# Step 0's part of ten tiles' outputs: made beside the end of step 0 instead of among the outputs at the end

## The chip, the cores and the metric

The kernel runs on one core of a Trainium2 chip. The metric is the device time of one execution in microseconds (us). PE is the matrix engine, PEld its weight loads, DVE, ACT and POOL are the vector, scalar and GpSimd engines, SP is the queue that issues most loads and stores.

## The reference

The input is x (3327 rows of 256, float32) and a sparse 0/1 matrix adj. Two layers follow each other, each with a residual and a layer norm. Layer 0 is a graph attention over adj with a gated update. Its normalised output X is what the change is about, for layer 1 does two steps from it:

```python
Z = 0
Xf = Xa = X
for n in range(2):
    A = top_p_attention(Xa)        # softmax of q k^T, the largest entries up to 0.9 of the sum kept
    Xf = R @ Xf                    # R: (adj + I), rows divided by their sums; sparse
    Xa = A @ Xa
    Z = Z + Xf @ U1[n].T + Xa @ U2[n].T
h = X + Z
out = layernorm(X + layernorm(h) * ln_g + ln_b)
```

So a row's sum before the first norm has five parts: X, two products from step 0 (Xf and Xa after step 0, with U1[0] and U2[0]) and two from step 1. Each part depends on that row alone, once Xf and Xa of the step are known.

## The kernel before

The 3327 rows are 26 tiles of 128 (the last has 127). In time the kernel has these stages: layer 0 (to about 398 us), step 0 of layer 1 (to about 966), step 1 (its products of A and Xa run from 988 to 1568), and the ends (1570 to 1833), where the outputs are made.

**Step 0** (`step_0`) is a pipeline over tiles. A tile's work is a generator, `sparse(t)`, and each call of it is a tick. A new tile enters every EVERY0 = 32 ticks (about 19.4 us in the steady part), and the table ORDER_0 says at which tick of a tile each part stands, from "logits0" at 0 to "qk3" at 180. So some six tiles are in work at once. Parts that matter here, with their names in the profile:

- "xf": the sparse product R X of a tile: POOL gathers the neighbours' rows (`g`), PE sums them (`pxf`), ACT scales to `xf`, SP stores it in `xf_rows` in DRAM.
- "index" and "needed": POOL gathers the rows of X with their keys that the tile needs (`g<-x1k,uidx`), after a small list has gone to DRAM and back (`ulist`, `back`).
- "turned": PE turns the gathered keys (`pk`), ACT copies them (`kg`). "by_nodes weights": PE makes the logits again for these few rows (`plt`), ACT takes the exponential (`w`). "kept": DVE removes those under the limit. "attention": PE sums (`pav`), DVE inverts the sum (`rA`). "xa": ACT writes the tile's Xa into `self.xa`, which holds all tiles in SBUF, and SP stores it in `xa_rows`.
- "qk": PE turns xa (`ptq`) and makes q and k of step 1 (`pq`), ACT copies them.

When the last tile has entered, the pipeline drains. Beside the drain a second generator, `first_1`, makes the logits and the largest entries of step 1's first tile as soon as the k that they need exist (`pl` on PE, copied by ACT).

**Step 1** works through the 26 tiles as dense products of the masked A and Xa (`pt`, `at`, `pav` on PE).

**The ends** (`ends`) have two kinds of work. A few "hard" rows, put aside because their limit needs an exact search, are done in three rounds: a search and a mask on DVE (`bound`, `hard`; the tiles with an h in their names), then transposes `pth`, copies `ath`, products `pavh` and the rows' own outputs `xh` (`hard_end`). Among these stand the outputs of the 26 tiles, one generator `tile_end(t)` each. A tile end loads the tile's Xf and Xa of both steps and X (`xfs`, `xa`, `x`), turns them on PE (`ptxut` for step 0, `ptxvt` for step 1: four transposes each), copies them on ACT (`xtut`, `xtvt`), makes the products on PE into one bank (`pzt`: four for `xtut`, four for `xtvt`, each as two halves U1, U2; then x1 by the identity, `plus`), and hands it to the two norms on DVE, ACT and POOL (`bn..`, `mv..`, `shift..`, and `h`, which lies in columns of qT that are free by then). A new tile end starts at 0.8 per tick; while DVE searches, PE works at tile ends.

On PE, DVE and ACT the order of the instructions is the order in which the program issues them (`manual_schedule`), in step 0 on POOL too. Everything else, SP's queue of loads and stores in particular, is put in order by a scheduler. Each engine takes its instructions strictly in its order.

U1 and U2 are loaded once (`load_u1`, for U1: `kT<-in_U1T_dram`), into columns of kT that step 0's logits have used before. The call stands after step 1's first mask; in SP's queue the scheduler had put it just after the last reading of those columns, and it is issued at 878.56 us.

Buffers that count: PSUM has two banks with the tag "av" (`pav`, `pzt`) and two with "sm" (`ptq`, `pk`, `ptxut` and other small ones); SBUF has two of tag "xf" (rows of Xf and Xa loaded from DRAM), two of tag "own" and four of tag "xt".

Of the kernel before, what the change touches and what calls it, by code (L numbers as in the profile page):

```python
# [9 lines left out]
F32 = mybir.dt.float32  # L10
# [6 lines left out]
P = 128  # L17
N = 3327
D = 256
DC = D // P  # L20
DA = 64
NT = (N + P - 1) // P
# [44 lines left out]
EVERY0 = 32  # L67
# [19 lines left out]
    ) for name in names.split()  # L87
]
AT_0 = {name: tick for tick, name in ORDER_0}

GROUP = (208, 167)
LIST = (40, 72)
# [14 lines left out]
def rows(t):  # L107
    return TAIL if t == NT - 1 else P
# [13 lines left out]
def move_rows(engine, dst, src, r):  # L122

    full = r // 16 * 16
    for a, b in ((0, full), (full, r)):
        if a < b:
            engine.dma_start(dst[a:b], src[a:b])
# [170 lines left out]
class SlowLayer1:  # L298
# [33 lines left out]
    def transposed(self, srcs, r, tag):  # L332

        nc = self.nc
        xt = self.work.tile([P, 2 * DC, P], F32, tag="xt", name=f"xt{tag}")
        pt = self.psm.tile([P, 2 * DC, P], F32, tag="sm", name=f"ptx{tag}")
        for s, a in enumerate(srcs):
            for c in range(DC):
                nc.tensor.transpose(pt[:, s * DC + c, :r], a[:, c * P : (c + 1) * P], self.ident[:r, :r])
        m = len(srcs) * DC  # L340
        nc.scalar.copy(xt[:, :m, :r], pt[:, :m, :r])
        return xt
# [827 lines left out]
class Layer1:  # L1170
# [52 lines left out]
    def setup_0(self, keep, dram):  # L1223
# [16 lines left out]
        self.needed = keep.tile([P, NT], F32, name="needed")  # L1240
        self.ulist = dram.tile([NT, UB * P], F32, name="ulist")

    def sparse(self, t):


        parts = self.parts_0(t)
        at = 0
        for tick, name in ORDER_0:
            while at < tick:
                at += 1  # L1250
                yield
            parts[name]()
# [319 lines left out]

    def step_0(self):

        tiles, first = [], self.first_1()
        self.done = self.phase = 0

        for p in self.p:
            self.nc.vector.memset(p.bitcast(BF16)[:, N : N + 1], -1.0)
        while self.phase < EVERY0 * NT or tiles:  # L1580
            if self.phase % EVERY0 == 0 and self.phase // EVERY0 < NT:
                tiles.append(self.sparse(self.phase // EVERY0))
            for g in list(tiles):
                if next(g, True):
                    tiles.remove(g)
                    self.done += 1
            next(first, None)
            self.phase += 1
        for _ in first:
            pass  # L1590

    def first_1(self):


        while self.phase <= EVERY0 * (NT - 1) + max(AT_0[k] for k in ("sign0", "sign1", "xf")):
            yield
        v = self.item(NT)
        self.item(NT + 1)
        self.fetch(NT)
        v.cand = self.candidates(v.r, GROUP[1], v.tag)  # L1600
        ready, waiting = [], list(range(-(-N // GROUP[1])))
        for pair in self.chunks():
            while self.done * P < min(NT * P, HALF + pair[0][1] + LC):
                yield
            for i in (NT, NT + 1):
                self.some_logits(i, pair)
                yield
            ready += [c for h, s in pair for c in range(h * HALF + s, min(N, h * HALF + s + LC))]
            have = set(ready)
            for g in list(waiting):  # L1610
                if have.issuperset(range(g * GROUP[1], min(N, (g + 1) * GROUP[1]))):
                    waiting.remove(g)
                    self.eights(v.cand, v.l, v.r, GROUP[1], g * GROUP[1], min(N, (g + 1) * GROUP[1]))
            yield

    def transposed(self, srcs, r, tag, kind="xt"):

        nc = self.nc
        xt = self.work.tile([P, 2 * DC, P], F32, tag=kind, name=f"xt{tag}", bufs=4)
        pt = self.psm.tile([P, 2 * DC, P], F32, tag="sm", name=f"ptx{tag}")  # L1620
        for s, a in enumerate(srcs):
            for c in range(DC):
                nc.tensor.transpose(pt[:, s * DC + c, :r], a[:, c * P : (c + 1) * P], self.ident[:r, :r])
        m = len(srcs) * DC
        nc.scalar.copy(xt[:, :m, :r], pt[:, :m, :r])
        return xt

    def chunks(self):

# [263 lines left out]
        yield  # L1893
        self.normalized(h, h, m, r, f"b{tag}")

    def tile_end(self, t):

        nc, r, sh = self.nc, rows(t), self.sh
        on = slice(t * P, t * P + r)
        a = self.work.tile([P, EB, P], F32, tag="m", name=f"xfs{t}").rearrange("p b c -> p (b c)")  # L1900
        xa2 = self.work.tile([P, D], F32, tag="xf", name=f"xa2_{t}")
        x1 = self.work.tile([P, D], F32, tag="xf2", name=f"x1_{t}")[:r]

        spare = lambda k: sh.qT[:r, k * D : (k + 1) * D]
        h, xb = spare(t % 9), spare(9 + t % 3)
        move_rows(nc.sync, a[:r, :D], sh.xf_rows[on, :], r)
        move_rows(nc.sync, a[:r, D : 2 * D], sh.xf2_rows[on, :], r)
        move_rows(nc.sync, xa2[:r], sh.xa2_rows[on, :], r)
        move_rows(nc.sync, x1, sh.x1_rows[on, :], r)
        yield  # L1910
        xts = [
            self.transposed((a[:r, :D], self.xa[:r, t, :]), r, f"ut{t}"),
            self.transposed((a[:r, D : 2 * D], xa2[:r]), r, f"vt{t}"),
        ]
        yield
        pz = self.pac.tile([P, 512], F32, tag="av", name=f"pzt{t}")
        for n, xt in enumerate(xts):
            self.output_terms(pz, xt, n, (0, 1), r, n == 0, False)
        self.plus(pz, x1, r)
        yield  # L1920
        rest = self.output_rows(pz, [xb], h, r, f"t{t}")
        for k, _ in enumerate(rest):
            if k == 2:
                move_rows(nc.sync, xb, sh.xb_rows[on, :], r)
            yield
        move_rows(nc.sync, self.out[on, :], h, r)
# [255 lines left out]
    def ends(self, bounds):  # L2182


        ends, open_ends, queue = [self.tile_end(t) for t in range(NT)], [], []
        ticks = 0

        def tick():


            nonlocal ticks
            ticks += 1
            if ends and (NT - len(ends) < 0.8 * ticks or not searching):
                open_ends.append(ends.pop(0))
            for g in open_ends[::-1]:
                if next(g, True):
                    open_ends.remove(g)

        def more():
            if queue and next(queue[0], True):  # L2200
                queue.pop(0)
            tick()

            for _ in range(2):
                for g in bounds:
                    if not next(g, True):
                        break

        def start(k):
            yield from self.hard_q(k)  # L2210
            for pair in self.chunks():
                yield
                self.hard_exp(k, pair)
            bounds.append(self.coarse_bound(k, CUTS[:COARSE], self.items[f"h{k}"].other))

        def end(k):
            yield from self.hard_end(k)
            open_ends.append(self.items[f"h{k}"].end)

        queue.append(start(2))  # L2220
        searching = True
        for k in range(HARD):
            if k:
                for _ in bounds[k - 1]:
                    pass
                for _ in self.bound(k, CUTS[COARSE:]):
                    more()
            for _ in self.hard(k):
                more()
            queue.append(end(k))  # L2230
        searching = False
        while queue or open_ends or ends:
            more()
        for k in range(HARD):
            self.hard_store(k)

    def run(self):
        nc, sh, total = self.nc, self.sh, STEPS * NT
# [4 lines left out]
        with self.tc.manual_schedule(engines=engines):  # L2243
# [5 lines left out]
            self.list_3(NT)  # L2249
            self.mask(NT)  # L2250
            self.put_aside_1(NT)
            self.load_u1()
            for i in range(NT, total):
                if i + 2 < total:
                    self.item(i + 2)
# [140 lines left out]
```

## Time and profile before

| | us |
|---|---|
| median of 3 runs | 1832.16 |
| lowest, highest | 1831.43, 1836.68 |
| the profiled execution | 1834.81 |
| its span | 1833.0 |
| PE busy (share of the span) | 1554.1 (85%) |
| DVE busy | 1396.6 (76%) |
| POOL busy | 1074.6 (59%) |
| ACT busy | 1056.6 (58%) |
| xa of tiles 23, 24, 25 written from | 943.45, 953.69, 963.98 |
| last copy of the hard rows' sum (xh) | 1795.79 |

The mean clock that PE was granted is 0.926 of full speed. The profile's other times are those of the one profiled execution, from the start of its span. In a line of the timeline stand the start, the length, the engine, the line of the program, the operation with its output and inputs, the number of instructions, and in brackets the engine's idle time before it with what it waited for.

### The profile page before, as it was taken

The numbers are of one execution on the slowest core, as the hardware profiler recorded it, in microseconds if no ns is written. First come the engines' busy times: TensorE is split into PE (matmuls) and PEld (weight loads), VectorE is DVE, ScalarE is ACT, GpSimd is POOL, SyncE is SP. The second block draws the span as 40 slices with busy tenths as digits, with TensorE's granted clock in tenths as the row PEclk, the third lists the DMA queues.
The fourth block names the chain that finished last, engine by engine and source line by source line (L and its number), as shares of the span: only waits on it lengthen the run. The fifth ranks groups of instructions, "written<-read, shape, count | busy, mean of one in ns | idle before, by whom it ended". The sixth has DMA issues, their size and how long they took to land. (4 is left out here: it accounts for less than half of the span.)

```text
span 1833.0 us, 28746 instructions
## 1 busy us (share of the span) xinstructions
PE 1554.1 (85%) x8425; PEld 1086.2 (59%) x8425; DVE 1396.6 (76%) x4759; ACT 1056.6 (58%) x2388; POOL 1074.6 (59%) x1774
## 2 busy tenths in 40 slices
PE   6499999976888898888766999999999889788992
PEld 4255555543555555555444777777777656677872
DVE  5788887447787788778628999999999877967741
ACT  3366666745667676766624555555555546558454
POOL 2477777624565566565463656665665583666654
PEclk9799999977899889889888999999999999899996
DMA  8877773322333333333330111111111120213321
GB/s 263 288 262 234 238 229 97 83 67 75 93 98 100 92 92 97 101 89 97 88 82 24 50 52 52 51 48 50 47 47 50 50 64 18 75 58 96 104 86 43
DMA packets 113861, 180.06 MB, mean 98 GB/s; under 512 B 27740, under 2 KB 82773, under 8 KB 113696
## 3 DMA queue, kind: packets, MB, share of 16 engines
q0 software_dynamic: 26624, 74.64, 15.7%
q1 hardware_dynamic: 68818, 86.65, 14.6%
q10 hardware_dynamic: 18254, 16.86, 2.7%
q8 instruction: 69, 1.13, 0.3%
q14 instruction: 96, 0.79, 0.1%
HBM read 146.08 MB, written 32.09 MB: 97 GB/s over the span
## 5 line engine op out<-in xcount | busy, mean ns | idle before, releaser
L1855 PE MATMUL pav<-xa,at 128*128 128x256 f32 (+2 forms) x1352 | 329.4, 388 | 7.3 <-ACT at L1841 7.3
L1855 PEld LDWEIGHTS pav<-xa,at 128*128 128x128 f32 (+2 forms) x1352 | 244.7, 190 | 86.6 <-ACT at L1841 40.4
L1654 DVE MAX8 cand<-array 128x8 f32<-128x167 f32 (+5 forms) x921 | 241.4, 336 | 28.8 <-ACT array L1641 20.7
L1641 ACT COPY array<-pl 128x416 f32<-128x416 f32 (+3 forms) x402 | 183.6, 509 | 132.5 <-PE pl L1638 114.7
L1638 PE MATMUL pl<-kT,qT 64*128 64x416 f32 (+3 forms) x804 | 228.7, 611 | 15.7 <-issue 8.0
L645 POOL DMA_INDIRECT g<-xf_rows,edge x130 | 136.3, 1048 | 165.5 <-PE pxf L1798 124.4
L645 POOL DMA_INDIRECT g<-x_rows,edge x130 | 137.4, 1057 | 86.4 <-issue 34.2
L1841 ACT COPY at<-pt 128x512 f32<-128x512 f32 (+2 forms) x182 | 96.0, 542 | 136.8 <-PE pt L1839 89.5
L645 POOL DMA_INDIRECT g<-whx,edge x130 | 140.7, 1082 | 47.0 <-issue 36.2
L1489 POOL DMA_INDIRECT g<-x1k,uidx x130 | 137.7, 1059 | 40.0 <-issue 38.9
L1672 DVE MAX8 lst<-cand 128x8 f32<-128x160 f32 (+3 forms) x364 | 113.5, 312 | 8.1
L1638 PEld LDWEIGHTS pl<-kT,qT 64*128 64x128 f32 (+1 forms) x804 | 77.8, 202 | 67.2 <-issue 34.0
L862 DVE FIND_INDEX8 at<-ones,array 128x8 uint32<-128x840 f32 (+1 forms) x104 | 105.5, 1027 | 0.0
L1770 DVE MATCH_REPLACE8 array<-gone,array 128x3335 f32<-128x3335 f32 (+1 forms) x26 | 94.0, 3617 | 0.0
L1674 DVE MATCH_REPLACE8 cand<-lst,cand 128x160 f32<-128x160 f32 (+3 forms) x312 | 92.9, 298 | 0.0
L1790 POOL TENSOR_SCALAR m<-col,erow 128x128 f32<-128x128 f32 x130 | 76.5, 602 | 1.0
L983 PE MATMUL acc<-g,m 128*128 128x259 f32 (+1 forms) x260 | 64.9, 397 | 6.8 <-ACT m L979 6.8
L1550 PE MATMUL pav<-g,w 128*128 128x257 f32 (+1 forms) x260 | 65.7, 398 | 5.4 <-DVE w L1544 4.7
L1798 PEld LDWEIGHTS pxf<-g,m 128*128 128x128 f32 (+1 forms) x260 | 49.4, 198 | 34.7 <-issue 24.8
L1798 PE MATMUL pxf<-g,m 128*128 128x256 f32 (+1 forms) x260 | 65.9, 403 | 3.1 <-DVE base L1961 3.1
L1550 PEld LDWEIGHTS pav<-g,w 128*128 128x128 f32 (+1 forms) x260 | 48.1, 194 | 28.0 <-DVE w L1544 12.8
L1484 POOL TENSOR_SCALAR uidx<-back 128x5 uint32<-128x5 f32 x26 | 7.1, 272 | 96.0 <-DMA back<-ulist 95.9
(556 smaller groups left out, 3872.6 us busy)
## 6 DMA issues: line engine op xcount, KB each, us to landing
array<-in_adj_dram SPq DMA_DIRECT2D x23, 1248.0 KB
array<-in_adj_dram SPq DMA_DIRECT2D x23, 415.5 KB
xf_rows<-xf SPq DMA_DIRECT2D x50, 128.0 KB
xa_rows<-xa SPq DMA_DIRECT2D x50, 128.0 KB
xfs<-xf_rows SPq DMA_DIRECT2D x50, 128.0 KB
whx<-table ACTq DMA_DIRECT2D x25, 129.5 KB
x_rows<-x ACTq DMA_DIRECT2D x25, 128.0 KB
x1k<-x ACTq DMA_DIRECT2D x25, 128.0 KB
```

What stands on the lines that cost most here:

```text
L645: self.nc.gpsimd.indirect_dma_start(out=dst[:, b, :], out_offset=None, in_=table[:, :], in_offset=bass.IndirectOffsetOnAxis(ap=self.edge[: ...
L862: nc.vector.max_index(at[:r, g, :], self.ones8[:r], ad[:r, g, :])
L1489: nc.gpsimd.indirect_dma_start(out=v.g2[:, b, :], out_offset=None, in_=sh.x1k[:, :], in_offset=bass.IndirectOffsetOnAxis(ap=v.idx[:, b : b ...
L1550: nc.tensor.matmul(v.acc[:r, : D + 1], v.w[:, b, :r], v.g2[:, b, : D + 1], start=(b == 0), stop=(b == UB - 1))
L1638: nc.tensor.matmul(pl[:r, :w], q[on], self.sh.kT[on, n, s : s + w], start=True, stop=True)
L1641: nc.scalar.copy(l[:r, h * HALF + s : h * HALF + s + w], pl[:r, :w])
L1654: self.nc.vector.max(cand[:r, g * 8 : g * 8 + 8], src[:r, g * group : min(N, (g + 1) * group)])
L1672: nc.vector.max(lst[:r, k : k + 8], cand[:r])
L1770: nc.vector.match_replace(rev, gone[:r], rev, -BIG)
L1798: nc.tensor.matmul(acc[:r, :D], v.m[:, b, :r], v.g[:, b, :], start=(b == 0), stop=(b == EB - 1))
L1841: nc.scalar.copy(at[:, :full, :r], pt[:, :full, :r])
L1855: nc.tensor.matmul(v.acc[: v.r, :D], at[:k, j - 4 * g, : v.r], V[:k, j, :], start=(j == 0), stop=(j == NT - 1))
```

## The change

For the tiles 0 to 9 the parts of step 0 and X are summed already while step 0 drains, and kept in DRAM (`z0_rows`); the tile end then loads that in place of X, and adds to it only step 1's two products.

- A new generator, `early_ends`, gets one call per tick of `step_0`. It waits for step 0's last logits, calls `load_u1`, loads Xf of two tiles (`xfe`), and then takes two tiles every 32 ticks, five times: transposes on PE (`ptxet`), copy on ACT (`xtet`), the products and X on PE (`pze`), copy to `z0_` on ACT, store. `turns` gives the place of each within the 32 ticks: 2, 3, 4, 24, 28 for the first tile of a pair (transposes, next load, copy, products, store) and 17, 18, 19, 25, 29 for the second.
- In the ends the tiles come in the order 10 to 25, then 0 to 9. The last ten are without `ptxut`, `xtut`, their four products and the load of Xf of step 0.
- `load_u1` is called in `early_ends`, no longer after step 1's first mask. In SP's queue its place is the same as before.

In the order of the compiled program the new instructions stand on PE so (`|` parts them; the numbers are tiles):

```
pc 24 | ptxet 0 | pxf 25 | pp 24 | ptq 21 | pq 21 | pk 22 | ptxet 1 | plt 22 | pu 24 | pxf 25
      | pze 0 | first logits | pze 1 | first logits | pav 22 | pc 25
ptxet 2 | pp 25 | ptq 22 | pq 22 | pk 23 | first logits | ptxet 3 | plt 23 | pu 25 | pze 2 | pze 3 | pav 23
ptxet 4 | ptq 23 | pq 23 | pk 24 | ptxet 5 | plt 24 | pze 4 | pze 5 | pav 24
ptxet 6 | ptq 24 | pq 24 | pk 25 | ptxet 7 | plt 25 | pze 6 | pze 7 | pav 25
ptxet 8 | ptq 25 | pq 25 | last of the first logits | ptxet 9 | pze 8 | pze 9
```

On ACT the copies xtet 4, 6 and 8 stand just before xa of tiles 23, 24 and 25, the odd ones after the exponential w of the tile, and the copies of z behind these. One of the two SBUF buffers "xf" is taken by `xf` of step 1's first tile from the second pair on, so that xfe 4 to 9 follow each other through the other one. On POOL the gathers and masks of step 1's second tile stand ahead of tile 24's key gathers.

```diff
+HALVES = 10
...
+        self.z0_rows = dram.tile([HALVES * P, D], F32, name="z0_rows")
...
     def step_0(self):
...
-        tiles, first = [], self.first_1()
+        tiles, first, early = [], self.first_1(), self.early_ends()
...
+            next(early, None)
             for g in list(tiles):
...
+    def early_ends(self):
+        nc, sh = self.nc, self.sh
+        while self.phase <= EVERY0 * (NT - 1) + AT_0["logits3"]:
+            yield
+        self.load_u1()
+        xfs, xts, pzs = {}, {}, {}
+
+        def load(t):
+            xfs[t] = self.work.tile([P, D], F32, tag="xf", name=f"xfe{t}")
+            move_rows(nc.sync, xfs[t][: rows(t)], sh.xf_rows[t * P : t * P + rows(t), :], rows(t))
+
+        def load_next(t):
+            if t + 2 < HALVES:
+                load(t + 2)
+
+        def transposes(t):
+            turn = self.transposing((xfs.pop(t)[: rows(t)], self.xa[: rows(t), t, :]), rows(t), f"et{t}")
+            next(turn)
+            xts[t] = turn
+
+        def copy(t):
+            xts[t] = next(xts[t])
+
+        def terms(t):
+            pzs[t] = self.pac.tile([P, 512], F32, tag="av", name=f"pze{t}")
+            self.output_terms(pzs[t], xts.pop(t), 0, (0, 1), rows(t), True, False)
+            self.plus(pzs[t], sh.x1[: rows(t), t, :], rows(t))
+
+        def store(t):
+            z = self.work.tile([P, D], F32, tag="own", name=f"z0_{t}")
+            nc.scalar.copy(z[: rows(t)], pzs.pop(t)[: rows(t), :D])
+            move_rows(nc.sync, self.z0_rows[t * P : t * P + rows(t), :], z[: rows(t)], rows(t))
+
+        load(0)
+        load(1)
+        at = {}
+        for i, turns in enumerate(((2, 3, 4, 24, 28), (17, 18, 19, 25, 29))):
+            at.update(zip(turns, [(i, f) for f in (transposes, load_next, copy, terms, store)]))
+        while self.phase % EVERY0 != 5:
+            yield
+        for t in range(0, HALVES, 2):
+            for k in range(EVERY0):
+                if k in at:
+                    i, f = at[k]
+                    f(t + i)
+                yield
...
-    def tile_end(self, t):
+    def tile_end(self, t, j):
...
-        h, xb = spare(t % 9), spare(9 + t % 3)
-        move_rows(nc.sync, a[:r, :D], sh.xf_rows[on, :], r)
+        h, xb = spare(j % 9), spare(9 + j % 3)
+        steps = (0, 1) if t >= HALVES else (1,)
+        if 0 in steps:
+            move_rows(nc.sync, a[:r, :D], sh.xf_rows[on, :], r)
...
-        move_rows(nc.sync, x1, sh.x1_rows[on, :], r)
+        move_rows(nc.sync, x1, (sh.x1_rows if 0 in steps else self.z0_rows)[on, :], r)
...
-        for n, xt in enumerate(xts):
-            self.output_terms(pz, xt, n, (0, 1), r, n == 0, False)
+        for n, xt in zip(steps, xts):
+            self.output_terms(pz, xt, n, (0, 1), r, n == steps[0], False)
...
-        ends, open_ends, queue = [self.tile_end(t) for t in range(NT)], [], []
+        ends = [self.tile_end(t, j) for j, t in enumerate((*range(HALVES, NT), *range(HALVES)))]
+        open_ends, queue = [], []
...
-            self.load_u1()
             for i in range(NT, total):
```

The helper `transposed` is split: `transposing` issues the transposes, and after a yield the copy.

## The prediction

> **What bounds the kernel now.** I read the slices first, for where PE is full and where it isn't, then the windows around the two stages that the change touches, then PE's timeline there.
>
> ```profile
> PE   6499999976888898888766999999999889788992
> DVE  5788887447787788778628999999999877967741
> PEclk9799999977899889889888999999999999899996
> ```
>
> A slice is 45.8 us. Step 0 lies in slices 9 to 22, step 1's products in 22 to 35, the ends in the rest. Slices 20 and 21 (871 to 962) are the drain of step 0: no new tiles enter and PE falls to 7 and 6. The change takes work out of the ends and puts it into the drain, so two questions decide: is the drain's idle time idle where the new work stands, and is PE what the ends wait for?
>
> ```profile
> 870.00:900.00 30.00, 22.95 (x169) 14.91 (x168) 23.64 (x109) 21.11 (x41) 15.79 (x18) 0.90 0.42 116
> 900.00:930.00 30.00, 20.79 (x115) 12.42 (x115) 9.34 (x37) 10.55 (x22) 15.80 (x18) 0.73 0.25 63
> 930.00:960.00 30.00, 23.26 (x124) 13.81 (x123) 3.96 (x13) 9.25 (x28) 17.13 (x21) 0.86 0.32 82
> ```
>
> Columns: stretch, length, busy us of PE, PE's loads, DVE, ACT and POOL, clock, DMA share, GB/s. PE is idle for 23.0 of these 90 us, and nobody else is full. It looks like free room. The timeline of PE says otherwise:
>
> ```profile
> 926.03 0.69 PE L1510 MATMUL pk<-ident,g 128*64 128x128 f32 x2 [3.98 <-DMA g<-x1k,uidx]
> 929.07 0.42 PE L1512 MATMUL pk<-ident,g 128*64 128x128 f32 x1 [2.35 <-DMA g<-x1k,uidx]
> ...
> 934.83 2.50 PE L1525 MATMUL plt<-diag,ones 128*128 128x384 f32 x4
> ...
> 946.71 1.48 PE L1525 MATMUL plt<-diag,ones 128*128 128x384 f32 x4
> 948.12 0.93 PE L1531 MATMUL plt<-qT,kg 64*128 64x128 f32 x10
> 950.77 2.44 PE L1550 MATMUL pav<-g,w 128*128 128x257 f32 x10 [1.71 <-DVE w L1544]
> 954.22 0.44 PE L658 MATMUL ptq<-ident,xa 128*128 128x128 f32 x2 [1.01 <-ACT xa L1563]
> 955.17 0.71 PE L668 MATMUL pq<-xtq,wkqk 128*128 128x128 f32 x4 [0.52 <-ACT xtq L661]
> ```
>
> From 929 on PE runs one tile after the other, each ptq, pq, pk, plt, pav, and xa on ACT. The xa of tiles 23, 24 and 25 stand at 943.45, 953.69 and 963.98: a cycle of 10.27 us, in which PE idles only 1.0 + 0.5 + 0.5 + 1.7. Behind the last xa everything is serial (last logits at 966.1, the list on DVE to 978, first product at 988), so what the drain grows by, the whole of step 1 is late by. The one long hole, 920 to 929, is POOL's: it had waited for tile 25's xf to be in DRAM.
>
> ```profile
> 912.03 1.01 POOL L645 DMA_INDIRECT g<-xf_rows,edge  x1 [10.62 <-DMA xf_rows<-xf]
> ```
>
> In the ends PE is busy 73.0 of the 80 us from 1720 to 1800, but not always as the limit: the mask of the third hard round sits on DVE, and ACT has its own queue.
>
> ```profile
> 1755.35 3.65 DVE L2117 SCALAR_TENSOR_TENSOR array<-array,th 128x3327 f32<-128x3327 f32 x1
> 1758.93 0.08 DVE L2117 DVE_READ_ACCUMULATOR array<-array,th 128x1 f32 x1
> ...
> 1765.21 1.04 PE L1839 MATMUL pth<-ident,array 128*128 128x128 f32 x8
> ...
> 1765.85 1.07 ACT L1841 COPY ath<-pth 128x512 f32<-128x512 f32 x2
> ```
>
> The mask ends at 1759.0; PE comes to its transposes (pth) at 1765.2, because tile ends stand before them. So PE is the limit there by 6.2 us and no more.
>
> **What the Trainium skill says.** "TensorE: Matmul & The Clock Gate", section "What's actually happening": the clock is halved by default and full only after a window of sustained work. The trace agrees: where PE was busy 1.62 of 5 us (925 to 930) the clock was 0.50, and plt above took 2.50 us against 1.48 at clock 1.00. So the price of the new matmuls in the drain depends on the clock. "DMA: Bandwidth & Descriptors", section "Latency and other measured facts": a fixed cost of about 2 us a transfer. It agrees: a load of xf rows issued at 1751.21 let PE go at 1753.45, 2.24 us. "Perfetto Trace Analysis", section "Optimization Strategy", advises interleaving regimes with different limits; that is what is done here, and the cycle above is the doubt.
>
> **The change part by part.** The prices are from the ends before: one tile's four transposes (ptxut) 0.43 us from start to start, its eight products by U1 and U2 (pzt from xtut) 1.73, the added x1 (pzt<-x,ident) 0.43; ACT's copy of the transposes 0.58 (0.49 apart), of z 0.39.
>
> *Taken from the ends.* Ten tiles lose 0.43 + 1.73 = 2.16 us of PE, 21.6 in all, ten ACT copies and ten loads of 128 KB; their x1 becomes z0, the same size. The order of the tiles is turned to 10..25, 0..9, so that all ten stand behind 1720 on PE. What counts lies on two stretches. Before pth of the third hard round 15.5 us of PE go (eight of the ten sets of transposes, seven of products). PE then waits for the mask at 1759.0 instead of arriving at 1765.2, but ACT's ath stands behind normalisations that POOL paces (the power that the last of them needs ends at 1762.1), so ath comes near 1763.0, not 1765.85: 2.85. The mask itself may come 1 us sooner, as DVE waited 3.77 and 1.31 us for ACT (bnah at 1726.84, mvat at 1729.11), and ACT has one copy less before each. From pth to the last output of the hard rows PE is full (1766 to 1793); 2 x 0.43 + 2 x 1.73 = 4.3 go. The tail after xh (1795.79 to the end) is POOL's and stays. Gain 2.85 + 1 + 4.3 = **8 us**. Bounds: 4, if ACT and POOL hold ath where it is and the 4.3 alone remain; 12.5, if ACT never holds it (6.2 + 1 + 4.3, and a little of the tail).
>
> *Added to the drain.* Each tile gets 0.43 + 1.73 + 0.43 = 2.59 us of PE, 25.9 for ten, one ACT copy of 0.58 and one of 0.39, a load and a store. They go in pairs, each function at a fixed tick, hence at a fixed place on PE, in the midst of the cycle:
> - Tiles 0 and 1: one set of transposes ahead of pxf of tile 25, one ahead of plt of tile 22, at the clock there 0.69 each (the price of ptq at 895), and two ACT copies before xf of tile 25, of which I take 0.3. Xf's store, POOL's gathers and pk of tile 23 behind them move by 0.69 x 2 + 0.3 = 1.7. The products go between logits before 920 and delay nothing on the path: the hole of 6.3 us to 929 covers their 4.3 (5 to 8 at the low clock; without that cover they cost all of it).
> - Tiles 2 and 3: transposes of 3 before plt of tile 23, 0.6. Both products between pu of tile 25 and pav of tile 23: 2 x 2.16 = 4.3, less 0.79 idle before pav, plus 0.9 for a clock of 0.64 to 1.00: 4.4. The copy xtet4 stands on ACT just before xa of 23: 0.6. Sum 5.6.
> - Tiles 4 and 5, and 6 and 7, alike: transposes of the odd one 0.43, both products ahead of pav 4.3 less the 1.7 idle = 2.6, a copy ahead of the next xa 0.6: 3.6 each, 7.2. Transposes of the even one fill the wait for xa.
> - Tiles 8 and 9: their products stand behind the last logits, where PE idles from 968.3 to beyond 975: nothing. Xtet9 on ACT is ahead of the exponentials, which have 2.3 us (ACT's idle before e at 976.14); it costs only past that.
>
> Cost 1.7 + 5.6 + 7.2 = **14.5 us**. Bounds: 8, if ACT's copies cost nothing and the filled holes keep the clock up (plt of tile 23 and what follows it had lost some 2 us to it); 20, if the products of 2 and 3 run at half clock (another 4) and every serial load costs 0.5.
>
> *Queues.* The loads xfe4 to xfe9 share one buffer, as the other is held by step 1's first xf: each waits on SP for the transposes of the tile before, some 3.5 us before its own transposes, against 2.24 for a load. I take nothing for it; its cover is 1 us, and past that plt waits. Behind them in SP's queue stand the xa stores and the list of tile 25's nodes (ulist, back), needed by POOL only after pk of 24, itself later by then. On POOL the five gathers and five masks for step 1's second tile now stand before tile 24's key gathers, which lands these 4.3 us later, as late as PE is: nothing. The load of U1 moves in the text, but keeps its place behind step 0's last logits (issued at 878.56 in the profile): nothing, and if it landed later only the products of tile 0 would wait.
>
> **Sum.** On the profiled execution, span 1833.0 and 1834.81 with what lies around it: 1834.8 + 14.5 - 8 = 1841.3. That execution is 2.65 above the median of 1832.16, so the same step gives 1838.7.
>
> **Rivals.**
> 1. The drain hides the work. For it: 23 us idle in 90 against 25.9, and DVE and ACT mostly free; a kept-up clock pays back. Against: PE takes its instructions in order, and the holes in the cycle are 1.7 where 4.3 are put. With the low cost of 8 and the high gain of 12.5: 1828; were the cost only the 3 us of ACT copies and first transposes, 1823. This is the one on the other side: its place is the wait for w before pav of tiles 23 to 25, its price 2.6 to 4.4 each, and the result turns faster than before where the three together cost under 3 or the ends pay more than the drain takes.
> 2. Waits grow in the drain: loads through one buffer, low clock. Cost 20, gain 6: 1846. For it: a clock of 0.50 from 925 to 935 and a load latency near its cover.
> 3. The ends aren't PE's: DVE and POOL hold them, gain 4, cost 14.5: 1843. For it: DVE is busy 19.24 of 20 us from 1740 to 1760, and POOL paces ACT. Against: PE is full from 1766 to 1793.
> 4. The change doesn't do what it says: U1 is loaded where it was. It costs nothing either way; the rest does take effect.
>
> **Numbers.** A measurement tells about 0.3% here, 5.5 us. Chances: the forecast (1832 to 1843) 0.58; rival 1 0.14; rival 2 0.13; rival 3 0.15. The forecast lies on both sides of 1837.7, about half and half. Predicted 1838.5; the range 1826 to 1847 leaves out most of rival 1's better half and 2's worse. Faster 0.13, same 0.32, slower 0.55.
>
> **What would show it.** In the profile after: a cycle of about 14 us between the xa of tiles 23, 24 and 25, PE with no idle before those pav, the last xa near 978 rather than 964; in the ends pth of the third hard round at about the mask's end, and 8 us less from the last product to the end. A cycle still near 10.3 refutes the cost; a stretch from the first product to the end shorter by over 12 refutes the gain. PE waiting for a load before ptxet is rival 2.

## The result, and the profile after

| | before | after |
|---|---|---|
| median of 20 runs, us | 1831.8 | 1835.6 |
| ratio, 95% interval | | 1.0016 (1.0004 to 1.0028) |
| span of the profiled execution | 1833.0 | 1834.2 |
| xa of tiles 23, 24, 25 | 943.45, 953.69, 963.98 | 939.73, 953.19, 966.64 |
| last copy xh | 1795.79 | 1796.46 |

The changed kernel is slower by 0.16%, 3 us. It was forecast 6 us slower (1838.5 against a median before of 1832.2), in a range of 1826 to 1847. Run again with the experiments below, on another occasion, the ratio was 1.0020 (1.0007 to 1.0033).

The slices of the page after, PE and its clock:

```profile
PE   6489999976898888888788999999999989788972
PEclk9799999987989898989988999999999999899986
```

The drain (slices 20 and 21) now has 7 and 8 where it had 7 and 6. The windows of the drain, with the columns of before:

```profile
870.00:900.00 30.00, 24.43 (x190) 17.21 (x189) 21.80 (x95) 20.32 (x43) 10.92 (x12) 0.94 0.37 99
900.00:930.00 30.00, 21.68 (x104) 12.56 (x102) 8.93 (x34) 10.94 (x25) 20.98 (x26) 0.77 0.35 93
930.00:960.00 30.00, 26.97 (x173) 21.10 (x172) 2.63 (x8) 10.70 (x31) 11.17 (x12) 1.00 0.37 100
```

From 930 to 960 the granted clock is 1.00 where it was 0.86, and PE is idle for 3 us where it was for 7. The timeline of PE in one cycle shows the order that the prediction spoke of:

```profile
945.48 1.13 PE L1933 MATMUL pze<-kT,xtet 128*128 128x256 f32 x4
946.45 1.03 PE L1933 MATMUL pze<-u,xtet 128*128 128x256 f32 x4
947.31 0.59 PE L1992 MATMUL pze<-x,ident 128*128 128x256 f32 x2
947.74 1.03 PE L1933 MATMUL pze<-kT,xtet 128*128 128x256 f32 x4
948.61 1.03 PE L1933 MATMUL pze<-u,xtet 128*128 128x256 f32 x4
949.47 0.59 PE L1992 MATMUL pze<-x,ident 128*128 128x256 f32 x2
949.90 2.33 PE L1554 MATMUL pav<-g,w 128*128 128x257 f32 x10
```

There is no bracket ahead of pav: the wait for w (1.71 us before) is filled, and 4.42 us of products stand in it. And the ends, PE first, then DVE and ACT at the third hard round:

```profile
1756.28 0.66 PE L1684 MATMUL ptxvt<-ident,xfs 128*128 128x128 f32 x2 [3.58 <-DMA xfs<-xf_rows]
...
1768.24 1.97 PE L1901 MATMUL pth<-ident,array 128*128 128x128 f32 x8 [5.87 <-DVE array L2179]
1770.03 3.45 PE L1917 MATMUL pavh<-xa,ath 128*128 128x256 f32 x8
```

```profile
1764.52 3.65 DVE L2179 SCALAR_TENSOR_TENSOR array<-array,th 128x3327 f32<-128x3327 f32 x1
1768.10 0.08 DVE L2179 DVE_READ_ACCUMULATOR array<-array,th 128x1 f32 x1
```

```profile
1769.39 0.59 ACT L1903 COPY ath<-pth 128x512 f32<-128x512 f32 x1 [6.19 <-PE pth L1901]
```

Pth stands at the end of the mask, 0.07 us behind it. PE waited 5.87 us for it, and before that 3.58 us for a load of rows (at its last load ahead of pth the kernel before waited 2.81). Then it is slow: from 1768 to 1774 the granted clock is 0.58, pth takes 1.97 us where it took 1.04, and the first pavh 3.45 where it took 1.99 (PE before):

```profile
1766.49 1.99 PE L1855 MATMUL pavh<-xa,ath 128*128 128x256 f32 x8 [0.24 <-ACT ath L1841]
```

The two profiles must not be taken off against each other from their starts. Tile 20's xa came 6.3 us sooner in the one after, ahead of anything that the change adds. That is scatter: in a kernel of the experiments whose step 0 is that of before (`e5_order_only`, on another chip of about the same speed) it comes at 868.33, 7.9 us sooner than in the profile before; and in the eight profiles of seven kernels taken on chips that are some 2% faster, it comes between 831.6 and 841.8. So I compare stages, each from an event of its own:

| stage, us | before | after | after again |
|---|---|---|---|
| xa of 20 to xf of 25 | 32.56 | 31.55 | 34.71 |
| xf of 25 to pk of 23's last wait | 20.27 | 20.02 | 20.01 |
| on to pav of 23 | 11.45 | 14.91 | 14.82 |
| pav of 23 to 24, 24 to 25 | 10.25, 10.29 | 13.45, 13.45 | 13.55, 13.44 |
| pav of 25 to last logits | 5.04 | 5.36 | 5.36 |
| on to step 1's first xa | 41.22 | 42.45 | 42.96 |
| on to the first xh | 649.49 | 652.71 | 649.58 |
| first xh to second | 69.63 | 70.33 | 69.08 |
| second xh to the mask's end | 32.56 | 33.97 | 33.40 |
| mask's end to pth | 6.21 | 0.07 | 0.07 |
| pth to the third xh | 30.58 | 28.22 | 28.40 |
| third xh to the end | 37.21 | 37.74 | 37.48 |

### The profile page after: what moved, and what is told of

It reads as the page before. It is cut to its first block, busy times and chain, and to the rows that moved or that the text cites. A ratio compares the mean times of both kernels' runs of the same rounds, so it can differ in the third digit from the quotient of the medians.

```text
span 1834.2 us, 28832 instructions
## 1 busy us (share of the span) xinstructions
PE 1566.7 (85%) x8445; PEld 1093.6 (60%) x8445; DVE 1398.3 (76%) x4759; ACT 1060.3 (58%) x2398; POOL 1076.7 (59%) x1774
## 5 line engine op out<-in xcount | busy, mean ns | idle before, releaser
L1554 PEld LDWEIGHTS pav<-g,w 128*128 128x128 f32 (+1 forms) x260 | 47.1, 189 | 21.6 <-issue 7.0
```

Of the source, the lines that this page charges most:

```text
L1554: nc.tensor.matmul(v.acc[:r, : D + 1], v.w[:, b, :r], v.g2[:, b, : D + 1], start=(b == 0), stop=(b == UB - 1))
```

## The experiments

Each ratio is to runs of the kernel before on the same chip and in the same session; some chips are 2% faster than others, so medians are not compared between sessions. The question was where the forecast 14.5 us of cost and 8 us of gain stand, and why the sum came out smaller.

**The early part alone** (`e1_early_only`).

```diff
-        steps = (0, 1) if t >= HALVES else (1,)
+        steps = (0, 1)
-        ends = [self.tile_end(t, j) for j, t in enumerate((*range(HALVES, NT), *range(HALVES)))]
+        ends = [self.tile_end(t, j) for j, t in enumerate(range(NT))]
```

> The early part in step 0 as in the change; the ends as before (all 26 tiles with both steps' products, in the order 0 to 25, X loaded as before), so z0 is made and not used. It measures the drain's cost alone. Theory: the two products ahead of pav of tiles 23, 24 and 25 are what costs: in the profiled pair the drain grew by 9.4 us from tile 21's xa to tile 25's, so 8 to 11 us over before, the last three xa 13.4 us apart, and the steady part of step 0 within its scatter of before. Rival, the change makes step 0 shorter ahead of the drain (tile 20's xa came 6.3 us sooner in the changed kernel's profile): then this kernel has that too and is 2 to 4 us over before.

Measured: 1.0052 (1.0034 to 1.0070), 9.3 us over before. The last cycles are 13.46 and 13.45 us. The theory holds; the rival of a shorter step 0 falls.

**The ends alone** (`e2_ends_only`).

```diff
-            next(early, None)
...
-        move_rows(nc.sync, x1, (sh.x1_rows if 0 in steps else self.z0_rows)[on, :], r)
+        move_rows(nc.sync, x1, sh.x1_rows[on, :], r)
...
+            self.load_u1()
```

> No early part; the ends as changed (10 to 25, then 0 to 9, the last ten without step 0's transposes, copy, products and load; they load X in place of z0, so step 0's two products of these ten tiles are left out). It measures the gain of the ends alone. Theory: the gain stops where PE has come down to DVE's mask of the third hard round; 6 to 8 us under before, PE idle for 5 us or more before pth. Rival, PE bounds the ends throughout: 21.6 us under before. Rival, DVE and POOL bound them: under 4 us.

Measured: 0.9950 (0.9930 to 0.9970), 9.0 us under before. From the first xh to the end it took 167.95 us, before 176.19. PE waits for the mask as in the whole change (timeline of PE):

```profile
1722.06 1.97 PE L1899 MATMUL pth<-ident,array 128*128 128x128 f32 x8 [6.20 <-DVE array L2177]
```

The 21.6 us that PE loses are not gained: the limit passes to DVE's mask. The two parts' ratios add up to 1.0002; the whole, 1.0016 and 1.0020, is within their intervals.

**Loads, transposes and copies without the products of tiles 2 to 7** (`e3_no_products`).

```diff
+                    if not (2 <= t < 8 and f in (terms, store)):
-                    f(t + i)
+                        f(t + i)
...
-        move_rows(nc.sync, x1, (sh.x1_rows if 0 in steps else self.z0_rows)[on, :], r)
+        move_rows(nc.sync, x1, (sh.x1_rows if 0 in steps or 2 <= t < 8 else self.z0_rows)[on, :], r)
```

> As the change, but tiles 2 to 7 have only their loads, transposes and copies xtet in the drain; their products, z and its store are left out, and their short tile ends load X (so step 0's products of six tiles are left out). Theory: the products ahead of pav are 8.5 us of the drain's growth, so the drain grows by about 1 and the kernel is 5 to 6 us under before, the last three xa 10.8 us apart. Rival, the loads through one buffer, the transposes and the copies ahead of xa are a large part: the xa stay over 12 us apart and the kernel is within 2 us of before.

Measured: 0.9981 (0.9967 to 0.9996), 3.4 us under before, less than the 5 to 6 expected; the interval (0.7 to 5.9 us) does not part the theory from its rival. The stages do: from xf of 25 to step 1's first xa it takes 103.0 us, where the three profiles with two sets of products in each wait have 109.6 to 110.1 and the four with the drain of before 98.5 to 104.1. So the products are most of the cost. The last two cycles, from pav to pav, are still 11.21 and 12.49 us, not 10.8 (the last three xa stand 11.3 and 14.2 apart), and on PE's timeline one pav is long:

```profile
907.02 2.44 PE L1554 MATMUL pav<-g,w 128*128 128x257 f32 x10 [1.71 <-DVE w L1548]
...
915.13 1.82 PE L1529 MATMUL plt<-diag,ones 127*128 127x381 f32 x4
...
919.51 4.12 PE L1554 MATMUL pav<-g,w 128*127 128x257 f32 x10 [1.71 <-DVE w L1548]
```

The same ten matmul instructions take 4.12 us where they took 2.44. The clock had fallen: over these 4.12 us the mean granted clock is 0.59, over the cycle before 1.00. The kernel with the ends alone, whose drain is that of before, shows it too:

```profile
905.61 2.32 PE L1529 MATMUL plt<-diag,ones 128*128 128x384 f32 x4
...
910.51 4.02 PE L1554 MATMUL pav<-g,w 128*128 128x257 f32 x10 [1.72 <-DVE w L1548]
```

So the profile of before, with 2.44 in all three, was a lucky draw. In it and in the three other profiles of the drain of before (two come below) pav of 23 to pav of 25 took 20.54, 24.77, 23.40 and 23.53 us, on the average 23.1. With two sets of products ahead of each pav it took 26.9 to 27.0 in all three profiles.

All profiles of this document agree on it. In the seven with nothing in the wait ahead of these pav, six have one or two of the three at 3.79 to 4.12 us, at a mean granted clock of 0.59 to 0.62. In the seven with something in that wait (one set of products, two, or the idle transposes that come last) all 21 take 2.33 to 2.44.

**The order alone** (`e5_order_only`): before, with `for j, t in enumerate((*range(10, NT), *range(10)))` and whole tile ends.

> The kernel before with one thing changed: the ends take the tiles in the order 10 to 25, then 0 to 9. Nothing is made early, every tile end is whole. Theory: the order by itself is worth nothing, within 0.3% of before. Rival: tile 25 with its 127 rows, and tile ends 0 to 9 that load rows stored long ago, change the ends by over 5 us one way or the other.

Measured: 0.9985 (0.9964 to 1.0006). No difference can be told; from the first xh to the end 175.85 us against 176.19.

**Six short tile ends, nothing made early** (`e6_ends_six`): the ends alone, with `HALVES = 6`.

> As the ends alone with ten short tile ends, but with six (0 to 5, at the end of the order): no early part, and step 0's products of six tiles left out, X loaded in place of z0. Theory: PE needs to lose only the 6 us by which it came after the mask of the third round, so six short ones gain what ten do, 7 to 9 us, and PE comes to pth at about the mask's end, with its clock up. Rival: each short tile end gains alike, so six gain 6/10 of ten's 0.5%, 5 us, and pth still comes after the mask by the same stretch as in the kernel before.

Measured: 0.9964 (0.9951 to 0.9977), 6.6 us under before. The interval holds both figures; the profile decides. Pth comes 1.6 us after the mask's end, not 6.2, at full clock, and the stage to the next xh is 27.76 us, shorter than with ten (28.30):

```profile
1764.41 1.04 PE L1899 MATMUL pth<-ident,array 128*128 128x128 f32 x8
1767.19 1.99 PE L1915 MATMUL pavh<-xa,ath 128*128 128x256 f32 x8 [1.74 <-ACT ath L1901]
```

Here PE waits for ACT's copy ath, which stands behind normalisations in ACT's queue: 1.74 us, where before it was 0.24. With ten short tile ends PE comes to pth earlier and waits for the mask instead, and its clock falls. From the second xh to the third it comes out alike: 69.35 us before, 61.9 to 62.3 in the four profiles with ten short tile ends, 62.0 to 62.2 in the five with six. (From the first xh to the end this one took 171.2 us, 5 less than before, which is also the rival's figure; but 1.6 of it are between the first and the second xh, ahead of every short tile end.)

**Six tiles, products behind the last logits** (`e4_six`, and again `e9_six_again`).

```diff
-HALVES = 10
+HALVES = 6
...
+        for t in range(2, HALVES):
+            k = EVERY0 * (t - 1)
+            at.update({k + 2: (transposes, t), k + 6: (copy, t)})
...
+        while not self.over:
+            yield
+        terms(2)
+        terms(3)
+        yield
+        store(2)
+        store(3)
+        terms(4)
+        terms(5)
+        yield
+        store(4)
+        store(5)
...
```

The flag `over` is set behind the last logits, and the generator is called again behind the first tile's exponentials and behind those of its list.

> Six tiles in place of ten. Tiles 0 and 1 as in the change; tiles 2 to 5 have their transposes in the wait for xa of tiles 22 to 25, the copy xtet behind that xa, and all their products behind the first tile's last logits, where PE waits for the list. The ends take 6 to 25, then 0 to 5. Theory: the drain grows by under 1.5 us, the ends gain as much as with ten tiles, as the mask on DVE is the limit either way, and some 2 more if PE keeps its clock up to pth: 6 to 9 us under before. Rival, the ends need all ten: gain 6/10 of it, 3 us under before. Rival, what stands behind the last logits delays the list or the first product: no faster than before.

> The six-tile version again (products of tiles 2 to 5 behind the last logits), beside the one that has one tile's products in each wait. By the stages of the profiles so far it should gain 7.2 us in the ends and pay nothing that stands out of the scatter in the drain: 5 to 9 us under before, 0.3 to 0.5%. Rival, the 0.7% measured on another chip is real: 12 us under.

Measured: 0.9930 (0.9906 to 0.9954), and again 0.9959 (0.9936 to 0.9983): faster than both kernels, by 7.4 us against before in the second, so the 12.6 of the first did not repeat. From the first xh to the end 168.7 and 168.5 us, as much gained as with ten; from xf of 25 to step 1's first xa 101.2 and 101.7 us, where the kernels with the drain of before have 98.5 to 104.1 and the change 109.6 and 110.1.

**One tile's products ahead of each pav** (`e8_one_each`, and again `e10_one_again`): as the last, with

```diff
+            if t < HALVES - 1:
+                at.update({k + 25: (terms, t), k + 29: (store, t)})
```

> As the version with six tiles, but with one tile's products ahead of pav of tile 23, of 24 and of 25 (tiles 2, 3, 4), and only tile 5's behind the last logits. Theory: one set of products is 2.16 us in a wait of 1.71, so 0.5 a tile, and a PE that is busy keeps its clock: the last three xa stand 10.8 us apart, none of their pav takes 4 us as in the kernels without products there, and the time is that of the six-tile version within 2 us. Rival: any product in that place costs its full 2.2 us a tile: 6 us more than the six-tile version.

> The version with one tile's products ahead of each of the last three pav, again. By its stages it gains 7.5 us in the ends and pays 1.8 at pav of tile 23: 5 to 7 us under before, within 2 us of the six-tile version. In the profile the last two cycles are again 10.6 us, at full clock. Rival, its products cost their whole time: 6 us behind the six-tile version.

Measured: 0.9976 (0.9961 to 0.9991) and 0.9964 (0.9950 to 0.9978). The second stood beside the six-tile version of 0.9959 (the first did not), so the products in the wait cost nothing that can be told. PE's timeline in the second:

```profile
904.42 1.13 PE L1946 MATMUL pze<-kT,xtet 128*128 128x256 f32 x4
905.39 1.03 PE L1946 MATMUL pze<-u,xtet 128*128 128x256 f32 x4
906.25 0.59 PE L2005 MATMUL pze<-x,ident 128*128 128x256 f32 x2
906.68 2.33 PE L1554 MATMUL pav<-g,w 128*128 128x257 f32 x10
```

The cycles are 10.62 us in both profiles. One set fits where two did not.

**The change again** (`e7_after`).

> The changed kernel again, on the chip of its parts. Theory: drain's cost and ends' gain add up, 0.52% less 0.50%, so within 0.3% of before, a little slower if anything. Rival, the two interact (what is late in the drain shifts loads in the ends): over 0.4% from before. In the profile the last three xa are again 13.4 us apart, and the stretch ahead of tile 20's xa differs from before by the scatter between executions, not by a fixed 6 us.

Measured: 1.0020 (1.0007 to 1.0033), cycles 13.55 and 13.44.

**The clock by itself** (`e11_warm`, and again `e12_warm_again`): before, with

```diff
+            for k in range(14 if t >= NT - 3 else 0):
+                nc.tensor.transpose(v.acc[:, :P], self.xa[:, k, :P], self.ident)
             for b in range(UB):             # the products of pav
```

> The kernel before with one addition: 14 transposes (1.5 us of PE, their output is overwritten by the products that follow) ahead of pav of tiles 23, 24 and 25, in the wait of 1.7 us for w. They compute nothing that is used. Theory: they keep the clock up, so none of the last pav takes 4 us and the last two cycles are 10.3 us each, 20.5 to 21 in all, against 23.4 to 24.8 in the three kernels with the drain of before that were profiled after it; some 2.5 us under before, which the times alone can hardly show. Rival, the long pav have another cause (the gathered rows come late): they stay, 23 us or more in all.

> The kernel with the 14 idle transposes ahead of each of the last three pav, again. Its first profile had the cycles at 10.2 us and no long pav, as the clock theory says, but its times were 0.2% over before (0.05 to 0.35%), where the theory says 0.1% under. If the 0.2% was chance, this is within 0.15% of before. If it is over before by 0.2% again, the transposes cost 3 to 4 us somewhere that the drain's stages do not show, and the clock kept up in the drain is no gain in the time.

Measured: 1.0020 (1.0005 to 1.0035) and 1.0025 (1.0011 to 1.0039). In the drain it does what it should (timeline of the first):

```profile
904.13 1.75 PE L1550 MATMUL pav<-ident,xa 128*128 128x128 f32 x14
905.91 2.44 PE L1552 MATMUL pav<-g,w 128*128 128x257 f32 x10
```

From pav of 23 to pav of 25 it is 20.4 us in both. But the kernel is slower, twice. In both profiles a loss stands elsewhere: from step 1's first xa to the first xh 654.3 and 654.5 us against 649.5, all of it in the last five tiles of step 1, where PE waits for DVE and POOL. The first such place, on PE's timeline of the first of these two, and then of before:

```profile
1401.61 3.84 PE L1800 MATMUL pxf<-g,m 128*128 128x256 f32 x10 [3.05 <-DVE base L1963]
```

```profile
1445.35 2.42 PE L1798 MATMUL pxf<-g,m 128*128 128x256 f32 x10 [3.06 <-DVE base L1961]
```

The same wait is followed by a low clock in the first (0.62 over the 3.84 us) and a full one in the second (1.00). It is not the filler's alone: the six-tile kernel had 653.6 us there in one execution and 649.5 in the other, and five of the twelve profiles without a filler have 650.8 us or more. Whether the filler makes it more frequent (by shifting when PE waits) or two profiles fell so by chance is **open**. So that the clock falls in the drain's waits, and that work in them prevents it, is shown by the profiles; that preventing it shortens the whole is not: taken by itself, it did not.

## Why the prediction was right, and where its sum was off

The sign, the place and the mechanism held: the last cycles went from 10.3 to 13.4 us (forecast about 14), pav had no idle before it, pth came to the mask's end, the ends gave 6 to 9 us. The net was half of what was forecast, 3 us for 6. The last xa stood at 966.64, not near the 978 that the prediction named as a sign: tile 20's xa happened to come 6.3 us sooner, and the cost was smaller.

- **The cost, 14.5 forecast, 9.3 measured** (e1, 6.1 to 12.6); by the profiles, from xf of 25 to step 1's first xa, 109.6 to 110.1 us in three against 101.5 on the average of the four with the drain of before, so 8.4. The term that was most oversized is that of tiles 4 to 7, 7.2. Against the one profile at hand it was nearly right: 3.2 a cycle (transposes 0.43, products 4.42 less 1.71, the copy ahead of xa 0.4, less 0.2 for a faster plt). But that profile's cycles of 10.3 were not typical. Against the average of the four (23.1 for two) both cost 3.8. I had put the clock into the lower bound as 2 us at tile 23 alone; the later waits were read as harmless because in that execution they were.
- Tiles 2 and 3, forecast 5.6 with the copy ahead of xa: the stage to pav of 23 grew by 3.5 against the profile before, by 3.8 against the average of four (11.17), and the copy added 0.4. The clock at plt was better than I assumed, and the 0.9 for a low clock was not paid.
- Tiles 0 and 1, forecast 1.7: their products cost nothing (20.27 and 20.02 us from xf to pk), as said; the stage ahead of it scatters between 27.5 and 34.7 us over all profiles, so the 1.7 is neither shown nor refuted.
- Tiles 8 and 9, forecast nothing: the stage behind the last logits grew by 1.2 to 1.7. The kernel without the products of 2 to 7 has those of 8 and 9 too and 41.22 us there, as before, and the filler kernel, without any, 42.4. So nothing shows that it is these products.
- **The gain, 8 forecast, 9.0 measured** (e2, 5.4 to 12.6); by the profiles, from the first xh to the end, 5.9 and 7.8 in the change and 8.2 in e2. The total was right by luck, for its parts were not. In the ten-tile kernel ACT did not hold ath: it waited 6.19 us for PE, and the whole of the 6.2 us was gained, where I took 2.85 (with six tiles ACT does hold it, by 1.74). Of the 4.3 behind pth 2.2 to 2.4 remained, as the cold clock after the wait took some 2.0 (0.5 from pth to pavh, 1.5 at pavh). The mask did not come 1 us sooner but 0.8 to 1.4 later. DVE's wait for xh ahead of it was 3.6 to 4.4 us in the four profiles with ten short tile ends and 3.77 before, so ACT's shorter queue did not show there; at the wait behind it 0.1 to 0.5 us were won (0.81 to 1.23 for 1.31). And in all four DVE's chain from bnah to the mask's end is longer, 33.0 to 33.6 us, where the ten other profiles have 32.2 to 32.4. It stands in a few short instructions, such as this one of DVE after, beside which POOL worked at a normalisation (the second line), and the same one of DVE before (the third):

```profile
1753.72 0.76 DVE L1830 TENSOR_SCALAR goneh<-goneh,th 128x8 f32<-128x8 f32 x1
1753.74 0.72 POOL L1950 TENSOR_TENSOR qT<-qT 128x256 f32<-128x256 f32 x1
1745.05 0.23 DVE L1768 TENSOR_SCALAR goneh<-goneh,th 128x8 f32<-128x8 f32 x1
```

In each of the four profiles three such instructions of DVE take 0.32 to 0.77 us instead of 0.20 to 0.23, and each ends within 0.05 us of the end of a 128x256 operation of POOL. No run tests whether POOL's operation is the cause.
- The rival that the drain hides the work was half alive: one set of products per wait is hidden, two are not. The rival of waits through one buffer fell: no transposes of the early part waited for a load in the cycles shown. U1's place was indeed of no effect that a stage shows.
- Two readings of the profile were off and moved nothing in the sum: PE's idle time in a cycle is 3.2 us, not 3.7 (the 0.5 stands there once), and the last logits keep PE busy until 969.6, so it idles from there and not from 968.3.

## What to carry to other kernels

Free time in a stage is free only at the places where it stands: count what fits into each wait on the path, here one set of products and not two. When work is taken off an engine, take only as much as brings it level with the next limit; six tiles gave what ten did, and cost nothing that the drain's stages show. A price from one profile holds for that execution's clock: before a wait is called harmless, look at it in several.

## What the runs showed that was not expected

The same ten matmuls of pav took 2.44 us in one execution and 3.81 to 4.12 in the others of kernels with the same drain, after waits of the same 1.0, 0.5 and 1.7 us. The stage from step 1's first xa to the first xh takes 649.4 to 649.6 us in seven of the fourteen profiles and 650.8 to 655.7 in the others, for the six-tile kernel and for the change once this and once that, while its first 20 tiles repeat to within 0.9 us; the difference arises in the last five, where PE has waits of 2 to 9 us. With ten short tile ends a few short instructions of DVE took 1.6 to 3.3 times as long while POOL worked at normalisations, and the mask came about 1 us later, though nothing had been added to DVE or POOL. And a filler that kept the clock up in the drain left the kernel 0.2% slower.
